# Repeated products at the kernel's begin: 12 of 512 columns in place of 23 of 256

## The chip, the cores and the metric

The kernel runs on one core of a Trainium2 chip. The metric is the device time of one execution in microseconds; the median of three runs stands for the kernel. One further execution was recorded by the hardware profiler, and every line of a profile below comes from such a recorded execution.

## What is computed

The input x is 16 images of 128 channels and 32 x 32 pixels, in float32. Two layers follow each other, and each has a mixing part and a feed-forward part, both added to their input:

```python
# layer 0
x = x + L0_conv(ln_c(x))      # linear attention, 4 heads of 32, over 1024 pixels
t = to_tokens(x)              # (16, 1024, 128)
t = t + L0_ffn(ln_t(t))       # spectral filters: long convolutions with 16 filters, two signs,
                              # each followed by a 128 x 128 matrix, plus 3 taps
# layer 1
x = x + L1_conv(ln_c(x))      # two 3 x 3 convolutions with batch norm and relu
t = t + L1_ffn(ln_t(t))       # routed experts: 64 experts, top 8 tokens each, 128 -> 512 -> 128
```

## The kernel before

The work is one long unrolled program with five stages that follow each other: attention and the forward transforms of layer 0 (to about 381 us), the product stage (to about 652 us), then the inverse transforms with the convolutions and the routing, then the experts, then the output.

The attention stage is a software pipeline over the 16 samples. A tuple `period` (L741) lists the steps of one period with the sample that each works on, written out by hand, and the engines' programs follow it in that order, since the stage is under a manual schedule. Transposes and products write PSUM tiles of the tags "big" (4 KB a partition, three buffers) and "s" (two buffers).

At some points of this order the kernel issues products whose result nobody reads: `keep` (L159) multiplies the identity with itself, repeated along the columns, into a PSUM tile `wm`. The table `idle` (L353) says after which step of which sample, and how many: nine after the `tokens` step of sample 1, eight after the first `filters` step, three after `channels` of sample 0 and three after `k` of sample 1, 23 in all. Two later stages call `keep` with the tag "cv": 26 products ahead of the inverse transforms, some between the routing steps, and four near the end.

The product stage forms, for each of 16 chunks of frequencies, the products of the filters' spectra with the input spectra. Its arrays and steps are:

- `generate(c, q)`: 16 small products (L816) of 32 rows into four PSUM banks `pg`, four times four, each in one of four row groups of PE; this makes a part of the filter matrix g of chunk c.
- `collect`: copies `pg` into `g`, on ACT (L829) and on DVE (L827).
- `multiply(c, m, x, py, fresh)`: 16 products (L840) of 128 rows and 32 columns of weights, g with the input spectra v, into the PSUM tile `py`.
- `turns(c, i)`: POOL prepares v from the loaded spectra xc (L807, L808).
- `combine` and `finish`: DVE and POOL form the result ys, and two transfers store it to yd in DRAM (L861).

In a chunk the loop over m runs four times. Each turn issues two `generate` of the next chunk, then two `multiply` of this one, so that PE alternates between a group of L816 and a group of L840. SP issues the loads of xc (L792, `fetch`) in each chunk: two after `generate` in the turn m = 0, one in m = 2 and one in m = 3. A float32 product is recorded in the trace as two matmul records and two weight-load records of PE, so a group of either line is 64 matmul records and 64 weight loads. The last chunk has no `generate`; then PE runs L840 alone.

The manual schedule of this stage holds for PE, DVE, ACT, POOL and SP: each engine takes its instructions in the order in which the code issues them.

Of the kernel before, what the change touches and what calls it, by code (L numbers as in the profile page):

```python
# [8 lines left out]
F32 = mybir.dt.float32  # L9
# [5 lines left out]
P = 128  # L15
# [54 lines left out]
def metaformer_kernel(ctx: ExitStack, tc: tile.TileContext, io: dict, out: bass.AP):  # L70
# [7 lines left out]
    ident = const.tile([P, P], F32, name="ident")  # L78
# [19 lines left out]
    for n, (g_, b_, m_, v_) in enumerate(((V_G1, V_B1, V_M1, V_V1), (V_G2, V_B2, V_M2, V_V2))):  # L98
# [15 lines left out]
                name=nc.get_next_instruction_name(), ins=[], outs=[], act_func_set_id=EXP_LN  # L114
# [43 lines left out]

    def keep(ps, tag, count):  # L159

        if count:
            wm = ps.tile([P, 2, P], F32, name="wm", tag=tag, bufs={"s": 2, "cv": 3}[tag])
        for _ in range(count):
            nc.tensor.matmul(
                wm, ident, ident.unsqueeze(1).to_broadcast([P, 2, P]), start=True, stop=True
            )

    def transpose_out(pt, src):
# [7 lines left out]
    with ExitStack() as l0:  # L176
# [43 lines left out]
        with ExitStack() as a0:  # L220
# [8 lines left out]
            ps = a0.enter_context(tc.tile_pool(name="aps", bufs=2, space=PSUM))  # L229
# [99 lines left out]
            for h in range(HEADS):  # L329
                s = slice(h * DH, (h + 1) * DH)  # L330
# [19 lines left out]
            def small(shape, name):  # L350
                return work.tile(shape, F32, name=name, tag=name, bufs=5)

            idle = {("tokens", 1): 9, ("filters", 0): 8, ("channels", 0): 3, ("k", 1): 3}  # L353

            class Attention:

# [401 lines left out]
            with tc.manual_schedule(engines=PINNED):  # L758
                for p in range(-reach, B):
                    next(preparing, None)  # L760
                    for name, d in period:
                        b = p + d
                        if name == "filters":
                            next(setting, None)
                            keep(ps, "s", idle.pop((name, 0), 0) if p > -reach else 0)
                        elif 0 <= b < B:
                            if name == "tokens":
                                samples[b] = Attention(b)
                            getattr(samples[b], "q_" if name == "q" else name)()
                            keep(ps, "s", idle.get((name, b), 0))  # L770
                assert next(preparing, None) is None
                for _ in setting:
                    pass
# [160 lines left out]
    with ExitStack() as c1:  # L934
# [6 lines left out]
        ps = cps.enter_context(tc.tile_pool(name="cps", bufs=2, space=PSUM, reuse_waits="tile"))  # L941
# [79 lines left out]
        idle = {(13, "turn"): 4, (13, "pooled"): 8, (15, "logits"): 11, (15, "turn"): 1}  # L1021
# [475 lines left out]
        with tc.manual_schedule(engines=PINNED | {mybir.EngineType.SP}):  # L1497
# [7 lines left out]
            for j in range(2):  # L1505
                nc.sync.dma_start(b2[j * E : (j + 1) * E, :], w2[:, HID, :])
            samples = [None] * B
            keep(ps, "cv", 26)
            for b, name in order:
                if name == "yin":  # L1510
# [128 lines left out]
        ps = c1.enter_context(tc.tile_pool(name="fps", bufs=4, space=PSUM, reuse_waits="tile"))  # L1639
# [175 lines left out]
```

## Time and profile before

| | us |
|---|---|
| median of three runs | 1238.39 |
| lowest and highest | 1237.03, 1242.1 |
| profiled execution, its own time | 1234.8 |
| its span | 1233.0 |
| PE busy, share of the span | 1160.1 (94%) |
| DVE, ACT, POOL busy | 935.7, 724.8, 604.0 |
| L816, PE busy | 142.7 |
| L840, PE busy | 126.7 |
| L164 (`keep`), PE busy, 154 matmul records | 35.1 |
| mean granted clock of PE | 0.991 of full speed |

The page gives the busy time of an engine as the union of its instructions, and for a group of instructions of one line the count, the mean duration of one, and the engine's idle time just ahead of them with what ended it. "issue" stands there when nothing that the profile shows, no semaphore and no transfer, ended it. The chain of waits follows the execution back from its last instruction and names at each step what released it. The timeline shows instructions in order of time, merged where they are alike, with the start, the length and the idle time ahead in square brackets. Of the DMA queues, q1 carries the kernel's own transfers; the queue q8 is called "instruction".

Four runs of L164 lie in the attention stage: they start at 10.50, 19.64, 26.93 and 42.47 us and have 18, 16, 6 and 6 matmul records. The product stage starts on PE at 382.20 us.

### The profile page before, as it was taken

How to read it: one execution, taken by the hardware profiler on the slowest of the kernel's cores; microseconds unless marked ns; L12 is line 12 of the kernel's file. 1: busy time of each engine (PE TensorE's matmuls, PEld its weight loads, DVE VectorE, ACT ScalarE, POOL GpSimd, SP SyncE). 2: the span in 40 equal slices, each digit the busy share in tenths (PEclk: the TensorE clock that was granted, in tenths of full speed). 3: DMA queues.
4: the chain of work that ended last, by engine and by line, in shares of the span. 5: the costliest groups of instructions: out<-in, count | busy, mean ns of one | idle time of the engine just before them, and what ended most of it. 6: DMA issues, size and time to landing. Idle time of an engine off the chain costs nothing.

```text
span 1233.0 us, 34413 instructions
## 1 busy us (share of the span) xinstructions
PE 1160.1 (94%) x14398; PEld 953.7 (77%) x14398; DVE 935.7 (76%) x1944; ACT 724.8 (59%) x1420; POOL 604.0 (49%) x800
## 2 busy tenths in 40 slices
PE   6889999999999999999988999999999999998996
PEld 5677767777777988888887888888888888886453
DVE  5888888888776777777764689898888989885235
ACT  4777787776655777777760445555555555644211
POOL 2436454655568789888882433343343333230003
PEclk9999999999999999999998999999999999999998
DMA  7005335253436243434338511233233321416899
GB/s 282 24 31 168 122 108 162 87 174 108 154 121 181 91 138 134 139 133 139 125 133 283 143 52 53 86 101 121 83 122 106 103 86 69 155 35 234 316 403 380
DMA packets 91243, 175.14 MB, mean 142 GB/s; under 512 B 5968, under 2 KB 42064, under 8 KB 90448
## 3 DMA queue, kind: packets, MB, share of 16 engines
q1 hardware_dynamic: 90448, 170.46, 41.0%
q0 software_dynamic: 640, 2.49, 0.7%
q8 instruction: 113, 1.85, 0.6%
q14 instruction: 42, 0.34, 0.1%
HBM read 110.28 MB, written 62.65 MB: 140 GB/s over the span
## 4 chain that ended last, share of the span: by engine, by line
PE 57%; DVE 22%; issue 11%; ACT 5%; DMA 4%; POOL 1%; SPq 0%; POOLq 0%; ACTq 0%; DVEq 0%
PE pg L816 10%; PE py L840 10%; PE pcv L1012 10%; PE big L638 7%; DVE bst L135 4%; PE big L171 3%; PE big L152 3%; PE big L570 3%; PE big L450 2%; PE big L533 2%; PE big L432 2%; DVE abss L1255 1%; DVE xp L1277 1%; DVE xp L1139 1%; ACT tt L144 1%
## 5 line engine op out<-in xcount | busy, mean ns | idle before, releaser
L1012 PE MATMUL pcv<-v,cw 128*128 128x256 f32 x1152 | 258.2, 380 | 0.8 <-POOL v L1202 0.8
L1012 PEld LDWEIGHTS pcv<-v,cw 128*128 128x128 f32 x1152 | 214.7, 190 | 33.9 <-issue 4.9
L829 ACT COPY g<-pg 128x512 f32<-128x512 f32 x316 | 161.1, 606 | 38.0 <-PE pg L816 37.3
L827 DVE COPY g<-pg 128x512 f32<-128x512 f32 x196 | 127.7, 681 | 68.3 <-PE pg L816 68.3
L816 PE MATMUL pg<-ph,mst 32*128 32x128 f32 x4096 | 142.7, 279 | 5.5 <-issue 4.5
L816 PEld LDWEIGHTS pg<-ph,mst 32*128 32x128 f32 x4096 | 127.9, 186 | 21.4 <-issue 10.7
L840 PE MATMUL py<-g,v 128*32 128x128 f32 x4096 | 126.7, 276 | 3.6 <-issue 2.1
L840 PEld LDWEIGHTS py<-g,v 128*32 128x32 f32 x4096 | 109.8, 111 | 11.7 <-issue 2.4
L144 ACT ACTIVATE tok<-tok,sts 128x128 f32<-128x128 f32 x256 | 101.9, 480 | 16.9 <-DVE sts L1089 13.6
L135 DVE BATCH_NORM_STATS2 bst<-big 128x6 f32<-128x256 f32 x256 | 91.0, 416 | 20.8 <-PE big L152 11.7
L807 POOL TENSOR_TENSOR v<-xc 128x256 f32<-128x256 f32 x128 | 99.9, 803 | 11.5 <-DMA xc<-vd 10.9
L638 PE MATMUL big<-u,mu 128*128 128x128 f32 (+4 forms) x384 | 86.0, 380 | 0.0
L1202 POOL TENSOR_TENSOR v<-abss 128x256 f32<-128x256 f32 x64 | 49.1, 787 | 68.2 <-DVE abss L1198 56.7
L286 POOL TENSOR_TENSOR xf<-ab 128x256 f32<-128x256 f32 x34 | 24.8, 728 | 110.5 <-DVE ab L253 110.5
L1221 POOL TENSOR_TENSOR yo<-abss 128x256 f32<-128x256 f32 x32 | 23.5, 734 | 108.5 <-DVE abss L1217 108.5
L638 PEld LDWEIGHTS big<-u,mu 128*128 128x128 f32 x384 | 56.7, 191 | 18.0 <-issue 15.4
L570 PE MATMUL big<-wf,ub 128*128 128x256 f32 x256 | 62.0, 385 | 0.2
L144 ACT ACTIVATE tt<-tt,sts 128x128 f32<-128x128 f32 x128 | 51.1, 480 | 14.5 <-DVE sts L1089 14.5
L808 POOL TENSOR_SCALAR v<-v 128x256 f32<-128x256 f32 x64 | 55.2, 863 | 5.6
L475 POOL TENSOR_TENSOR ke<-ke,ks 128x1024 f32<-128x1024 f32 x16 | 30.6, 1913 | 55.1 <-DVE qs L483 43.4
L570 PEld LDWEIGHTS big<-wf,ub 128*128 128x128 f32 x256 | 46.2, 190 | 8.8 <-ACT xn L423 3.0
L914 ACT COPY yt<-py 128x512 f32<-128x512 f32 x60 | 35.1, 585 | 27.9 <-ACT g L829 17.2
(256 smaller groups left out, 2488.4 us busy)
## 6 DMA issues: line engine op xcount, KB each, us to landing
we<-in_weight SPq DMA_DIRECT2D x32, 1024.0 KB, 8.9
xc<-vd SPq DMA_DIRECT2D x64, 256.0 KB, 3.2
yd<-ys SPq DMA_DIRECT2D x32, 512.0 KB, 3.5
vd<-xf SPq DMA_DIRECT2D x15, 1024.0 KB, 5.1
y<-yd SPq DMA_DIRECT2D x15, 896.0 KB, 6.2
x<-in_x SPq DMA_DIRECT2D x16, 512.0 KB, 5.2
mi<-in_M_phi SPq DMA_DIRECT2D x16, 512.0 KB, 4.7
xd<-x SPq DMA_DIRECT2D x16, 512.0 KB, 6.3
```

The costliest lines, as they stand in the source:

```text
L135: nc.vector.bn_stats(bst[:, j : j + 2, :].rearrange("p j s -> p (j s)"), src[:, j : j + 2, :].rearrange("p j c -> p c j"),)
L144: nc.scalar.activation(dst[:, j, :], src[:, j, :], AF.Identity, bias=nm[:, j : j + 1], scale=r[:, j : j + 1],)
L570: nc.tensor.matmul(dst, self.ub[:, q, :], wf[:, q, :], start=True, stop=True)
L638: nc.tensor.matmul(self.pa[:, a:hi], mu[:, NF - 1 - si, tap, :], self.u[:, a - tap : hi - tap], start=(tap == 0), stop=(tap == KU - 1),)
L807: nc.gpsimd.tensor_tensor(vv[:, x, 1:, bs], e, o, op)
L808: nc.gpsimd.tensor_scalar(v[:, :, 0, bs], v[:, :, 2, bs], -1.0, None, ALU.mult)
L816: nc.tensor.matmul(pg[r][:, i], mst[rs, 4 * q + i, :], ph[rs, c, :], start=True, stop=True,)
L827: nc.vector.tensor_copy(dst, src)
L829: nc.scalar.copy(dst, src)
L840: nc.tensor.matmul(py[rows, x, kl, :], v[:, (x * NM + m) * JL + jl, 1 - ri : 3 - ri, :] .rearrange("p k b -> p (k b)"), g[:, ((x * 2 + ri) ...
L1012: nc.tensor.matmul(pc[:, i], wt[:, dy, k, :], v[:, k, dy * WT : dy * WT + HT], start=(dy == 0), stop=(dy == 2),)
L1202: nc.gpsimd.tensor_tensor(v[:, k, WT : WT + HT], self.ab[:, 0], self.ab[:, 1], op)
```

## The change

The PSUM tile of `keep` and the columns of one product depend on the tag now: four times 128 columns with the tag "s", which the attention stage uses, and two times 128 with "cv", as it was. The table `idle` of the attention stage has 5, 4, 1 and 2 products in place of 9, 8, 3 and 3: 12 of 512 columns (6144 in all) in place of 23 of 256 (5888). The number of buffers of each tag is as before. In the program this takes away 11 products, 44 instructions of PE, ahead of the product stage; the other engines' instructions and their order are unchanged.

```diff
     def keep(ps, tag, count):
 
+        n, bufs = {"s": (4, 2), "cv": (2, 3)}[tag]
         if count:
-            wm = ps.tile([P, 2, P], F32, name="wm", tag=tag, bufs={"s": 2, "cv": 3}[tag])
+            wm = ps.tile([P, n, P], F32, name="wm", tag=tag, bufs=bufs)
         for _ in range(count):
             nc.tensor.matmul(
-                wm, ident, ident.unsqueeze(1).to_broadcast([P, 2, P]), start=True, stop=True
+                wm, ident, ident.unsqueeze(1).to_broadcast([P, n, P]), start=True, stop=True
             )
...
-            idle = {("tokens", 1): 9, ("filters", 0): 8, ("channels", 0): 3, ("k", 1): 3}
+            idle = {("tokens", 1): 5, ("filters", 0): 4, ("channels", 0): 1, ("k", 1): 2}
```

## The prediction

> **What bounds the kernel now.** I read the page's shares first, then its groups, then the chain of waits, then the timeline of the stage that the chain names. PE is busy 94% of the span and the chain is 57% PE, led by two lines of the product stage:
>
> ```profile
> PE 57%; DVE 22%; issue 11%; ACT 5%; DMA 4%; POOL 1%; SPq 0%; POOLq 0%; ACTq 0%; DVEq 0%
> ...
> L816 PE MATMUL pg<-ph,mst 32*128 32x128 f32 x4096 | 142.7, 279 | 5.5 <-issue 4.5
> ...
> L840 PE MATMUL py<-g,v 128*32 128x128 f32 x4096 | 126.7, 276 | 3.6 <-issue 2.1
> ```
>
> Their idle time is put down to "issue": PE had operands and buffers, and still did not go. The PE timeline shows where:
>
> ```profile
> 427.50 2.07 PE L816 MATMUL pg<-ph,mst 32*128 32x128 f32 x64
> 429.50 1.95 PE L840 MATMUL py<-g,v 128*32 128x128 f32 x64
> 431.38 2.07 PE L816 MATMUL pg<-ph,mst 32*128 32x128 f32 x64
> 433.38 1.96 PE L840 MATMUL py<-g,v 128*32 128x128 f32 x64
> 435.26 2.18 PE L816 MATMUL pg<-ph,mst 32*128 32x128 f32 x64
> 437.37 1.95 PE L840 MATMUL py<-g,v 128*32 128x128 f32 x64
> 439.25 0.94 PE L816 MATMUL pg<-ph,mst 32*128 32x128 f32 x20
> 440.38 0.84 PE L816 MATMUL pg<-ph,mst 32*128 32x128 f32 x20 [0.19 <-issue]
> ```
>
> One L816 group and one L840 group take 2.00 + 1.88 = 3.88 us undisturbed (427.50 to 431.38). The 439.25 group is broken after 20 products and reaches L840 at 441.92: 2.67 us instead of 2.00. The 435.26 group took 2.11. This repeats every chunk (four pairs): breaks at 424.08, 440.38, 456.69, 473.00, 489.31. From the L816 start at 399.68 to the one at 636.55 there are 58 pairs; 58 x 3.88 = 225.0 us, the trace shows 236.9, so **11.8 us are lost**, 0.81 a chunk.
>
> The broken places are periodic in the count of instructions. Numbering all PE records (products, weight loads, semaphore records) in order, every "issue" wait of the stage lies at number 193 or 194 modulo 256, while the start of the group drifts. The page has a queue that moves blocks of that size:
>
> ```profile
> q8 instruction: 113, 1.85, 0.6%
> ```
>
> 1.85 MB / 113 = 16 KB, and 28,981 PE records / 113 = 256. So PE's own instructions arrive in blocks of 256, and the stage eats a block in 3.88 us. The packet records give the delivery: a packet starts at least 1.05 us after PE has crossed into the block before, takes 0.97, and a stalled PE goes on 1.31 to 1.45 after it landed (landed 439.01, on at 440.38). But often it starts later, and then its start follows the kernel's transfers:
>
> ```profile
> 430.15 0.80 SPq L792 DMA_DIRECT2D xc<-vd  x2
> 434.29 0.80 SPq L861 DMA_DIRECT2D yd<-ys  x2
> 438.69 4.57 SPq L792 DMA_DIRECT2D xc<-vd  x2
> ```
>
> After a yd pair the block's packet starts 3.70 to 3.82 us behind the first issue (434.29 to 438.06) in nearly all chunks, although the crossing lay anywhere from 1.4 to 1.9 us behind it; after an xc pair 3.3 to 3.5; after a single xc about 2.2, mostly within the 1.05. Four packets, a chunk's worth, take 16.3 us, against 15.5 of PE work.
>
> [...] The windows view shows a mean of 0.91 over 60 to 70 us, behind the 2.72 us wait for wy at 67.33.
>
> **The change part by part.** (1) Products at the begin, L164 (46 of its 154 records). A 256-column product is two records 0.216 us apart; a 512-column one two at 0.45 (L432: four from 31.28 to 33.08). PE pays 46 x 0.216 = 9.9 us before and 24 x 0.45 = 10.8 after. None lies on the path: run 1 goes from 10.50 to about 15.0, phi lands at 15.98 (idle then 1.56); run 2 from 19.64 to 23.3, then gt until 24.25; run 3 shrinks 1.3 to 0.9 ahead of xn at 29.25; run 4 grows 1.3 to 1.8, from 42.47 to 44.3, ahead of gt at 44.74. 0 us. If that cover were gone, run 4 would cost 0.5. [...]
> (2) The wm tile grows to 2 KB a partition with the same two buffers. The instruction order of the two kernels is equal on DVE, ACT, POOL and SP, and on PE but for these rows, with the same waits: 0 us.
> (3) 11 products fewer are 22 matmul and 22 weight-load records: **every block boundary falls 44 records later in the work.** In the L816 group it moves from record 41 to 85 (early chunks) and from 27 to 71 (late ones; a few semaphore records shift it). Inside the group a record is 13.1 ns, so PE reaches the boundary 0.57 us later, while the yd and xc issues hang on the work and stay.
> Walk one undisturbed chunk, G = start of an L816 group. yd pair at G - 0.97, packet at G + 2.80, usable at G + 2.80 + 0.95 + 1.35 = 5.10, which is 1.22 into the next group. Before, PE is at the boundary 0.67 in: it waits. After, 1.24 in: the wait vanishes early; late (1.06 in) 0.16 is left. xc pair: issued G - 1.23, packet G + 2.2, usable 0.6 to 0.7 into the next group: even before, free after. The other two: crossing at 1.22 at the latest + 1.05 + 0.97 + 1.35 = 0.71 into the next group, free.
> A wait costs its length plus a restart of 0.2 to 0.3 (440.38: 0.37 longer than usual, 0.67 lost), a block just in time about 0.1 (435.26). So a chunk loses 0.1 early and about 0.4 late, mean 0.23, against 0.81. The same rule carried through the 58 pairs with their own packet times gives 11.7 before (trace 11.8) and 3.3 after. **Gain 8.4 us.**
> (4) Last chunk: the wait "issue" of 2.10 us before 647.30 ends with a packet that starts at 645.02 behind the loads of 639 to 641 (wi, 1024 KB, at 641.01). PE gets there 44 x 14.7 ns = 0.65 later: gain 0.65. It may also spare the half clock that follows it (0.89 over 636.6 to 652.4), at most 1.7; not counted.
> (5) Elsewhere: in the attention, convolution and expert stages a block lands 3.5 to 29 us before PE needs it. 0. The wait at 395.25 is followed by one for v (POOL, behind the xc loads) until 398.02, so shortening it gains 0.
> Sum 9.1 us. The profiled execution took 1234.8 us (span 1233.0 and 1.8 around it): 1225.7. It lies 3.6 under the median of the runs, 1238.4; that median becomes 1229.3.
>
> What is late next is POOL:
>
> ```profile
> core 0: us, PE busy (x) PEld busy (x) DVE busy (x) ACT busy (x) POOL busy (x), PEclk, DMA share, GB/s
> ...
> 457.00:473.30 16.30, 16.10 (x519) 14.64 (x516) 12.12 (x20) 12.52 (x24) 14.05 (x17) 1.00 0.40 133
> ```
>
> 14.05 of 16.30 us; a chunk of 15.6 still holds it, and the first pairs ran four times at 3.88 without a break.
>
> **Rivals.** *The fetch keeps a rhythm of its own* (four blocks in 16.3 us wherever the boundary lies): gain 0, 1238.4. For it: chunk and four blocks have the same period, so most chunks can't tell. Against: the constant distance to yd. *Gain taken up elsewhere*: if POOL's turns or the xc loads allow no chunk below 15.9, 0.4 x 14.5 = 6 is gained, 1232. Against: POOL waits 1.5 us a chunk for DVE's ys. *Not the count that decides*, or not 44: also 1238.4; the order listing speaks against it. *Slower*: a fetch asked for later runs into the next single xc (issued G + 3.0, just ahead of the next group) and waits for it: packet G + 5.2, usable 3.6 into the next group, a wait of 2.4, against 0.81 now; in all 14.5 chunks +23 us, 1261. It decides from about 5 chunks on. Against: that packet starts near G + 2.3, 0.7 us ahead.
>
> **How the numbers follow.** Forecast, or more: 0.68 (a gain over 6.2 us, which is 0.5%, about what a measurement of this kernel can tell from no change). Gain taken up: 0.12, own rhythm or wrong count 0.15, both within 0.5%; slower 0.05. Low end: all 11.8 and most of the last wait and its clock, 14.4, gives 1224; high end: no change and 1 us of spread, 1239.5.
>
> **What would show it.** Right: "issue" waits stay at the same number modulo 256 but lie some 40 products into L816; pairs mostly 3.88 us apart; the 58 pairs take about 228 us; L816's idle for issue falls. Wrong: breaks every 16.3 us as now; packets no longer tied to yd; PE idle in the stage for DVE, ACT or POOL; or a new idle in the first 60 us.

## The result, and the profile after

The median is 1232.87 us (20 runs, 1226.33 to 1240.06) against 1236.96 for the kernel before in the same comparison. The ratio is **0.9959, with an interval of 0.9943 to 0.9976**: 5.1 us gained, between 3.0 and 7.0. The forecast was 9.1 us. The profiled execution took 1229.23 us (span 1227.4) against 1234.8 (span 1233.0), 5.6 less. Line numbers below `keep`'s new line are one higher than before: L816 is L817, L840 is L841.

From the page of the kernel after, the shares of its chain of waits and the two groups of the product stage:

```profile
PE 54%; DVE 21%; issue 10%; ACT 6%; DMA 5%; POOL 2%; SPq 0%; POOLq 0%; ACTq 0%; DVEq 0%
...
L817 PE MATMUL pg<-ph,mst 32*128 32x128 f32 x4096 | 138.6, 278 | 1.1 <-DVE x L646 0.9
L841 PE MATMUL py<-g,v 128*32 128x128 f32 x4096 | 125.1, 274 | 2.4 <-POOL v L809 1.8
```

Before, 4.5 of the 5.5 us of idle time ahead of the first group and 2.1 of the 3.6 ahead of the second were put down to "issue"; now 1.1 and 2.4 us are left, most of it put down to DVE and POOL. PE's timeline at the place where the kernel before broke at 440.38, again start, length and idle time in brackets:

```profile
430.13 2.07 PE L817 MATMUL pg<-ph,mst 32*128 32x128 f32 x64
432.12 1.96 PE L841 MATMUL py<-g,v 128*32 128x128 f32 x64
434.01 2.17 PE L817 MATMUL pg<-ph,mst 32*128 32x128 f32 x64
436.11 1.95 PE L841 MATMUL py<-g,v 128*32 128x128 f32 x64
438.00 2.07 PE L817 MATMUL pg<-ph,mst 32*128 32x128 f32 x64
439.99 1.95 PE L841 MATMUL py<-g,v 128*32 128x128 f32 x64
```

No group is broken. One takes 2.17 in place of 2.07: its block of instructions had landed 1.46 us before PE went on in it, within the 1.24 to 1.48 us after which PE went on at the 18 gaps over 0.15 us that the kernel before has at block boundaries, so it came just in time. Later in the stage such groups stand close together:

```profile
568.10 2.22 PE L817 MATMUL pg<-ph,mst 32*128 32x128 f32 x64
...
572.14 2.38 PE L817 MATMUL pg<-ph,mst 32*128 32x128 f32 x64
...
576.34 2.33 PE L817 MATMUL pg<-ph,mst 32*128 32x128 f32 x64
```

From the L817 group at 399.08 to the last one at 628.29, 58 pairs, the stage takes 229.21 us in place of 236.87. At 3.8815 us for an undisturbed pair (3.88 in the prediction) the loss fell from 11.75 to 4.08.

**The last chunk** gained as well. Before:

```profile
641.05 4.15 PE L840 MATMUL py<-g,v 128*32 128x128 f32 x141 [0.54 <-DVE pooled L927]
647.30 5.13 PE L840 MATMUL py<-g,v 128*32 128x128 f32 x115 [2.10 <-issue]
```

After:

```profile
633.21 4.55 PE L841 MATMUL py<-g,v 128*32 128x128 f32 x155 [0.56 <-POOL v L809]
638.20 2.82 PE L841 MATMUL py<-g,v 128*32 128x128 f32 x93 [0.43 <-issue]
640.94 11.49 PE L165 MATMUL wm<-ident 128*128 128x256 f32 x52
```

The wait for instructions fell from 2.10 to 0.43, and the half clock behind it (granted clock 0.50 from 648.4 to 651.8 before) is not there (1.00 from 633.0 to 656.0). From the last L817 group to the L165 run (`keep` with "cv", behind the stage) it is 12.65 us in place of 15.81. With 0.6 gained ahead of the first pair, the stage ends 11.43 us earlier (640.94 against 652.37). Neither the 0.6 nor the 3.2 is firm: five more executions with the same count of PE records (experiments 2, 5, 6, 7 and 9) start the first pair 0.4 to 1.5 us later than the kernel before, and in experiment 2 the wait in the last chunk is back.

**The transition** to the convolutions then takes back 4.6 of these 11.4 us. The chain of waits before:

```profile
656.18 4.33 DMA yd<-ys
...
663.56 9.91 DMA cw<-cwd
673.48 9.95 DMA y<-yd
...
688.01 5.45 PE pcv L1012 x24
```

After:

```profile
644.77 7.31 DMA yd<-ys
...
655.11 10.50 DMA cw<-cwd
665.63 11.01 DMA y<-yd
...
681.20 5.45 PE pcv L1013 x24
```

The stage's last yd pair is issued 11.4 us earlier but takes 7.31 us to land instead of 4.33; SP issues nothing of what follows until then (its next transfer is at 652.53, before at 660.98). Then the loads of cw and y take 0.6 and 1.1 longer. The last line of each fence begins with the 13th matmul record of the convolutions, called the 13th record below; it starts only 6.8 us earlier. The windows view, from the begin of the L164 or L165 run to that record, before and then after (time, then busy time and count of PE, PEld, DVE, ACT and POOL, the granted clock, the share of the DMA engines, GB/s):

```profile
652.37:688.01 35.64, 29.82 (x169) 25.59 (x168) 19.55 (x40) 7.92 (x15) 11.29 (x15) 0.95 0.89 269
```

```profile
640.94:681.20 40.26, 29.87 (x171) 25.89 (x169) 19.98 (x40) 7.92 (x15) 11.30 (x15) 0.96 0.92 267
```

PE's work is the same, the rate is the same, each has one stretch of 3.4 us at half clock (granted clock 0.50 from 668.9 before, from 656.0 after), and there is more to move: 35.64 us at 269 GB/s is 9.59 MB, 40.26 at 267 is 10.75. The 1.16 MB more take 4.3 us at this rate, and the stretch is 4.6 longer. They are probably for the most part the loads of xp and y (1.4 MB) that POOL issues during the last chunk. POOL's timeline before and after:

```profile
646.51 0.62 POOL L1032 DMA_DIRECT2D xp<-xd  x1
647.13 0.69 POOL L1035 DMA_DIRECT2D y<-yd  x1
```

```profile
638.44 0.62 POOL L1033 DMA_DIRECT2D xp<-xd  x1
639.05 0.69 POOL L1036 DMA_DIRECT2D y<-yd  x1
```

Before, they are issued 5.9 us ahead of the stage's end and 9 ahead of the last yd pair (655.82); after, 2.5 and 6 us ahead (644.41). From the issue of the pair to its landing the DMA engines moved 1.1 MB before (233 GB/s from 655.8 to 660.5) and 2.05 after (270 from 644.4 to 652.0), and the pair itself is 1.05, so that it seems to share them with these loads for longer; experiment 9 tests that. From the 13th record on, the convolutions and the routing run alike (425.7 and 425.8 us to the last record of a convolution). Behind POOL's last step in the chain, which ends 6.85 us earlier (1217.39 against 1224.24), the program still runs 10.0 us instead of 8.8, and 5.6 us reach the end.

### The profile page after: what moved, and what is told of

Its sections match the earlier page's. It is cut to its first block, busy times and chain, and to the rows that moved or that the text cites. A ratio compares the mean times of both kernels' runs of the same rounds, so it can differ in the third digit from the quotient of the medians.

```text
span 1227.4 us, 34369 instructions
## 1 busy us (share of the span) xinstructions
PE 1154.2 (94%) x14376; PEld 945.1 (77%) x14376; DVE 930.1 (76%) x1944; ACT 725.1 (59%) x1420; POOL 601.0 (49%) x800
## 4 chain that ended last, share of the span: by engine, by line
PE 54%; DVE 21%; issue 10%; ACT 6%; DMA 5%; POOL 2%; SPq 0%; POOLq 0%; ACTq 0%; DVEq 0%
PE pg L817 10%; PE pcv L1013 10%; PE py L841 10%; PE big L639 6%; DVE bst L135 4%; PE big L172 3%; PE big L152 3%; PE big L571 3%; PE big L451 2%; PE big L534 2%; PE big L433 2%; DVE abss L1256 1%; DVE xp L1278 1%; DVE xp L1140 1%; ACT ub L550 1%
## 5 line engine op out<-in xcount | busy, mean ns | idle before, releaser
L817 PE MATMUL pg<-ph,mst 32*128 32x128 f32 x4096 | 138.6, 278 | 1.1 <-DVE x L646 0.9
L817 PEld LDWEIGHTS pg<-ph,mst 32*128 32x128 f32 x4096 | 125.9, 186 | 14.8 <-DVE g L828 8.3
L841 PE MATMUL py<-g,v 128*32 128x128 f32 x4096 | 125.1, 274 | 2.4 <-POOL v L809 1.8
L841 PEld LDWEIGHTS py<-g,v 128*32 128x32 f32 x4096 | 108.1, 110 | 10.6 <-POOL v L809 2.3
L808 POOL TENSOR_TENSOR v<-xc 128x256 f32<-128x256 f32 x128 | 97.0, 781 | 11.2 <-DMA xc<-vd 10.6
L1203 POOL TENSOR_TENSOR v<-abss 128x256 f32<-128x256 f32 x64 | 49.0, 786 | 68.2 <-DVE abss L1199 56.7
```

Source lines behind the costliest of these rows:

```text
L808: nc.gpsimd.tensor_tensor(vv[:, x, 1:, bs], e, o, op)
L817: nc.tensor.matmul(pg[r][:, i], mst[rs, 4 * q + i, :], ph[rs, c, :], start=True, stop=True,)
L841: nc.tensor.matmul(py[rows, x, kl, :], v[:, (x * NM + m) * JL + jl, 1 - ri : 3 - ri, :] .rearrange("p k b -> p (k b)"), g[:, ((x * 2 + ri) ...
L1203: nc.gpsimd.tensor_tensor(v[:, k, WT : WT + HT], self.ab[:, 0], self.ab[:, 1], op)
```

## The experiments

My theory was that the place of the 256-record boundaries in the work, and so the count of PE records ahead of the stage, decides the pairs, and that the transition is bound by bytes. The rivals: the size of the products or of the tile, a rhythm of the fetch's own, and PE's time in the last chunk. "Pairs" below is the time of the 58 pairs, and "entry" the time from the start of the last L817 group to the 13th record (51.46 before, 52.91 after). All ratios are to the kernel before. The diffs show the lines that matter; where a loop over `ticks` is added, a table gives its count behind each step. Times inside a kernel come from one execution of each.

**1. The count put back** in the kernel after, with products of one column: four behind `tokens`, three behind `filters`, four behind `channels`, so that the 11 products are there again and the columns hardly change.

```diff
+        for _ in range(ticks):
+            nc.tensor.matmul(wm[:, 0, 0:1], ident, ident[:, 0:1], start=True, stop=True)
```

> The changed kernel with 11 one-column products more at its begin: PE's columns and PSUM tile as after the change, the count of PE records ahead of the product stage as before it (boundary again at record 41 to 27 of the L816 group). If the count decides, the 58 pairs of the product stage take 236 to 238 us again and the time is that of the kernel before, ratio 0.998 to 1.002. If the wider products or the clock at the begin decide, the pairs take about 229 us and the ratio stays near 0.996. If the four blocks had a rhythm of their own, the pairs would show 16.3 us in four wherever the boundary lies.

Ratio 1.0005 (0.9989 to 1.0020); pairs 236.28. The breaks are back, at the same kind of place as in the kernel before; the page of this kernel:

```profile
L823 PE MATMUL pg<-ph,mst 32*128 32x128 f32 x4096 | 142.9, 279 | 4.4 <-issue 3.4
```

With the 44 records back the pairs take what they took before, so the gain hangs on the count, and neither the 512 columns nor the larger tile brings one. This kernel enters the stage 1.7 us later than the kernel before (383.91), which is in its ratio.

**2. Twelve products of 256 columns**, the other half of that test: the count of after, half the columns and the old tile.

```diff
-        n, bufs = {"s": (4, 2), "cv": (2, 3)}[tag]
+        n, bufs = {"s": (2, 2), "cv": (2, 3)}[tag]
```

> 12 products of 256 columns: the count of the changed kernel, half its columns. If the count decides: pairs near 229 us, product stage ended some 10 us earlier than in the kernel before, ratio 0.994 to 0.998 as after the change. If PE's work at the begin decides: another time[...].

Ratio 0.9958 (0.9942 to 0.9973), pairs 229.91: as the kernel after, although PE has 10.8 / 2 = 5.4 us less to do at the begin. This run tells something of the transition as well. In its last chunk the wait for instructions is back:

```profile
641.41 2.82 PE L841 MATMUL py<-g,v 128*32 128x128 f32 x93 [1.80 <-issue]
644.16 6.09 PE L165 MATMUL wm<-ident 128*128 128x256 f32 x27
```

So its stage ends 3.2 us later than that of the kernel after, 14.12 us behind the last L817 group in place of 12.65, and yet its 13th record starts at 681.20, the same as there.

**3. and 4. More records in the kernel before**, 28 and 13 products of one column (10, 8, 7, 3 and 5, 4, 4, 0 behind the four steps), the `ticks` loop as in 1. The boundary comes to lie in the L840 group, at record 57 to 43 with 28 and at 117 to 103 with 13.

> The kernel before with 28 one-column products more at its begin, 112 records: the boundary falls at record 57 to 43 of the L840 group (185 to 171 of the pair). The rule of the prediction gives no wait at all in the 58 pairs: 225 to 226 us, against 236.9 before and 229.2 after; ratio 0.990 to 0.995 if the gain is kept behind the stage. Added products cost nothing if the waits at the begin cover them, up to 3 us if not. If a boundary in the L840 group costs more than in L816, the pairs take longer than 229.

> The kernel before with 13 one-column products more, 52 records: the boundary falls at record 117 to 103 of the L840 group, just ahead of the single xc issue. The rule says that the request then runs into that transfer and the next block comes late: waits of over 1 us in every chunk, 58 pairs in 245 to 260 us, ratio 1.005 to 1.02, with 15 products less than the run beside it. If only the direction of the shift counted, or if the rule of the request and the transfers is wrong, the time lies between that of the kernel before and 0.4% below.

With 28: ratio 0.9944 (0.9925 to 0.9964), pairs 225.44, nothing but 0.3 us lost. It begins the stage 3.7 us late (385.87), since the added products take longer at the begin (2.29, 1.84, 1.62 and 0.72 us in their four runs) than the waits there cover and PE is at half clock for 3.4 us from 18.9 (the 16 records with phi take 5.39 us there, 3.69 before), and is still faster than the kernel before. With 13: **1.0107 (1.0083 to 1.0131), slower**, pairs 251.06. Its timeline:

```profile
442.95 1.93 PE L846 MATMUL py<-g,v 128*32 128x128 f32 x58
445.70 0.42 PE L846 MATMUL py<-g,v 128*32 128x128 f32 x6 [0.82 <-issue]
```

L846 is this kernel's L840. PE stops after 58 of the 64 records. With fifteen products of one column fewer than in 3 it is 20 us slower: a size of work can't do that, nor can a rhythm of the fetch's own, which would give all kernels the same pairs. The table that follows has this kernel's break at 445.70, behind a yd pair, but not all are of that kind: of the 32 gaps over 0.15 us between the two PE records at a block boundary in the 58 pairs (18 in the kernel before, 6 after), 14 have a single xc load as the transfer issued last ahead of the packet, 10 a yd pair and 8 an xc pair.

**The same block in six kernels.** From the packet records of q8 and the SP and PE timelines, for PE's record 8129, which is where the kernel before breaks at 440.38. "Into the block before" is when PE crossed the boundary before this one. Times but the last column count from the issue of the yd pair ahead of it:

| kernel | into the block before | packet starts | landed | PE reaches the boundary | PE's gap there, us |
|---|---|---|---|---|---|
| before | 1.63 | 3.77 | 4.72 | 5.63 | 0.46 |
| count back (1) | 1.63 | 3.79 | 4.72 | 5.51 | 0.67 |
| 13 added (4) | 1.14 | 4.06 | 5.00 | 5.15 | 1.09 |
| after | 2.19 | 3.65 | 4.61 | 6.08 | 0.09 |
| 24 added (8) | 0.09 | 1.38 | 2.31 | 3.88 | 0.09 |
| 28 added (3) | -0.14 | 0.07 | 1.30 | 3.65 | 0.09 |

0.09 is the usual distance of two groups of records. In this block the packet comes within 1.4 us of the yd issue when PE crosses up to 0.09 us behind that issue; where PE crosses 1.14 or more behind it, the packet starts 3.7 to 4.1 behind the issue, whether the crossing was 1.1 or 2.2 us behind it. Then it matters when PE wants the block: at 5.2 to 5.6 it waits, at 6.1 it doesn't. By the place of the boundary, from early chunks to late ones, the 58 pairs lose 11.8 us at L816 record 41 to 27, 4.1 at 85 to 71, 0.3 at L840 record 57 to 43, 0.2 at 73 to 59, and 25.9 at 117 to 103. So the change went most of the way down; the lowest losses measured lie 100 to 116 records further on (a pair has 256), and another 44 records on is the highest. No run kept the count and moved these transfers: that the packet follows them is read from these distances.

**5. PE slowed in the last chunk** of the kernel after by 16 products of 128 columns.

```diff
+                        for _ in range(4 if c + 1 == NCH else 0):
+                            nc.tensor.matmul(py[:, 0, 0, :], ident, ident, start=True, stop=True)
                         for x in range(2):
```

> The changed kernel with 16 products of the identity more in the last chunk, which nobody reads: some 3.5 us of PE time ahead of the last multiplies, about what the change gained in this chunk (12.65 us from the last pair to the end of the stage, against 15.81 before). If transfers bind from there on (the last yd pair lands behind the loads of xp and y that were issued 6 us ahead of it), the end of the stage moves 2.5 to 3.5 us later, the last yd pair lands in less than 7.3 us, the convolution starts (13th product of pcv, at 681.20 after the change) within 1.5 us of before this edit, and the ratio stays at 0.995 to 0.997. If the end of the stage decides, the convolution starts 3 us later and the ratio is near 0.999.

From the last L817 group to the L165 run it is 15.98 us, 3.3 more. The ratio is 0.9946 (0.9926 to 0.9966), not shown to differ from the kernel after, and entry is 52.32 in place of 52.91. The chain:

```profile
649.63 4.74 DMA yd<-ys
...
657.40 9.77 DMA cw<-cwd
667.18 10.37 DMA y<-yd
```

The yd pair lands in 4.74 again. The 3.2 us that the change gained in the last chunk bring nothing as far as the 13th record, as experiment 2 shows too: a stage that ends earlier only meets more of the loads.

**6. and 7. The loads of cw ahead of the others** on SP, in the kernel after, both of them in 6 and only the first in 7. The diff is that of 6:

```diff
+            for n in range(2):
+                nc.sync.dma_start(cw[n], cwd[n])
             for b in range(2):
                 load(b)
-            for n in range(2):
-                nc.sync.dma_start(cw[n], cwd[n])
```

> The changed kernel with both loads of cw (1152 KB each) issued by SP ahead of the loads of the first two samples, so that they no longer queue behind the wait for the last yd pair. If idle DMA time between yd and y costs the transition (57 and 95 GB/s in the two 2.5 us slices from 650 to 655), the convolution starts 1 to 4 us sooner and the ratio falls to 0.992 to 0.995. If sample 0's y, which then waits behind 2.3 MB, decides, the first product with wi comes 2 to 4 us later than 655.9 and the convolution starts 0 to 3 us later: 0.996 to 0.999. It can also be neither, when SBUF of cw comes free only at the stage's end.

> As the run with both cw loads first, but only cw0 is moved, cw1 stays behind the samples. If the idle DMA time is the cost, the 1152 KB fit into it and sample 0's y is hardly later: convolution 1 to 3 us sooner, ratio 0.993 to 0.995. If y of sample 0 or the transfers' own rate decides, no change: 0.995 to 0.997.

Ratios 0.9997 (0.9984 to 1.0009) and 0.9960 (0.9942 to 0.9979): the first loses the gain and lies above both ranges expected, the second shows no change. The chain of 6:

```profile
646.99 13.41 DMA yd<-ys
660.45 3.15 DMA y<-yd
```

cw is issued before the last yd pair now and goes through at its cost: the pair takes 13.41 us (10.79 in 7), and entry is 55.06 (51.56 in 7). The transfer that was moved ahead took its time from the next one.

**8. The kernel before with 24 cheap products**: as in 3, but with 32 columns of weights, and 8, 6, 7 and 3 of them: the eight behind `filters` took 1.84 us in 3, the eight behind `tokens` take 0.67 here.

```diff
+        for _ in range(ticks):
+            nc.tensor.matmul(wm[:32, 0, 0:1], ident[:, :32], ident[:, 0:1], start=True, stop=True)
```

> The kernel before with 24 products of 32 columns of weights and one column more at its begin, 96 records, shorter than those of the run with 28: the boundary falls at record 73 to 59 of the L840 group. By the rule no wait in the 58 pairs, 225 to 226 us as with 28, and the stage begins sooner than with 28 (385.87 there, 382.2 before). If the 58 pairs decide what the change is worth: ratio 0.990 to 0.994, below both the changed kernel and the run with 28. If the transition takes the rest back, 0.994 to 0.996.

Pairs 225.35; the stage begins at 382.22, as in the kernel before. Ratio **0.9919 (0.9887 to 0.9950)**, median 1226.96 (7 runs) against 1235.94: the lowest ratio of these kernels, 10 us below the kernel before (6 to 14), though its interval overlaps those of the others that gain. On its page neither group has issue as its main wait:

```profile
L846 PE MATMUL py<-g,v 128*32 128x128 f32 x4096 | 125.3, 274 | 3.1 <-POOL v L814 1.8
L822 PE MATMUL pg<-ph,mst 32*128 32x128 f32 x4096 | 135.1, 277 | 0.9 <-DVE x L649 0.9
```

Its last pair starts 11.65 us earlier than before (624.90), and the 13th record 8.8 (679.20): it pays at the transition as well (entry 54.30). It pays once more right behind that:

```profile
679.20 7.64 PE L1018 MATMUL pcv<-v,cw 128*128 128x256 f32 x24 [4.92 <-POOL v L1208]
```

The 24 records that took 5.45 us in the kernels before and after take 7.64, with PE at half clock for 6.8 us from 676.9 on, within the wait (the mean granted clock from 638.32 to the 13th record is 0.93, before 0.95). The last record of a convolution is then only 6.5 us earlier than before. So this execution, which ends 6.5 us before that of the kernel before and 0.9 before that of the kernel after, does not show the 10 us of the ratio.

**9. POOL's two loads moved to SP**, in the kernel after, so that they stand behind the last yd pair.

```diff
-            (nc.sync if b else nc.gpsimd).dma_start(xt[b], xd[b])
+            nc.sync.dma_start(xt[b], xd[b])
...
-                (nc.gpsimd if b + i == 0 else nc.sync).dma_start(
+                nc.sync.dma_start(
```

> The kernel after, with the loads of sample 0 that POOL issues (xp, and the first part of y) issued by SP instead, so that they stand behind the last yd pair and not ahead of it. PE's instructions and the product stage are unchanged: pairs about 229 to 231 us. Theory A (the last yd pair takes 7.3 us in the kernel after because these loads, issued 6 us ahead of it, share its transfer time): the pair lands in 4.3 to 4.8 us, SP goes on about 3 us earlier; but the bytes taken from ahead of it now follow it, so the 13th pcv product lies 51 to 55 us behind the last pair (52.9 in the kernel after), ratio 0.993 to 1.000. Rival B (the pair is long for another reason, such as its own size or the stage's other stores): it still takes about 7 us, SP's later loads start no earlier, and the 13th pcv product lies 3 us or more later, since xp and y now start 14 us later; ratio 0.998 to 1.003.

The chain:

```profile
645.81 3.94 DMA yd<-ys
649.81 6.77 DMA y<-yd
```

The pair takes 3.94 in place of 7.31, so these loads were what it shared with. Entry is 49.87, 3.0 better than after and a little better than either theory had it; the 10.85 MB from the L165 run to the 13th record go at 286 GB/s, where the kernel after moved 10.75 MB at 267. So the bytes alone do not set the length of this stretch: their order counts too. But the ratio is 0.9955 (0.9934 to 0.9976), as the kernel after. The table follows four kernels to the end, in us from the span's start:

| | last pair | 13th record | last record of a convolution | end of the span |
|---|---|---|---|---|
| before | 636.55 | 688.01 | 1113.74 | 1232.99 |
| after | 628.29 | 681.20 | 1106.97 | 1227.41 |
| POOL's loads on SP (9) | 630.06 | 679.93 | 1104.96 | 1229.81 |
| 24 added (8) | 624.90 | 679.20 | 1107.25 | 1226.47 |

In 9, the part behind the last convolution (experts and output) took 124.9 us, against 119.2 to 120.4 in the other three, with PE at half clock for 6.8 us from 1194.1 (mean granted clock 0.85 from 1180 to 1200; the other three are at 1.00 there and at 0.91 from 1120 to 1140, where 9 is at 1.00). Whether that follows from the order of the loads, or is the spread of single executions, stays open; so does what the 3.0 us are worth at the end.

## Why the prediction was right in kind and too large

**The mechanism held.** Experiments 1, 3 and 4 change the count of PE records by tiny products, and the pairs follow it from 225.4 to 251.1 us, in both directions; in experiment 2 the count stays, and so do the pairs. In the kernels that wait, the waits lie at the same record number modulo 256: 193 or 194 in the prediction, and the six gaps over 0.15 us that the kernel after has at block boundaries lie there too.

**Step 1 and step 2, nothing at the begin: right.** The product stage starts at 382.06 us, before at 382.20, and in experiment 2, with half the columns and the old tile, at 382.14. No half clock is added ahead of the stage, one is gone: the 0.91 of the prediction comes from a granted clock of 0.50 from 68.2 to 71.5, and after it is 1.00 from 60 to 70, although the wait for wy at 67.31 is 2.71 us long there too.

**Step 3, the pairs: 7.7 us measured, 8.4 predicted.** The walk through the packet times left a loss of 3.3, the trace shows 4.08. The first 28 pairs lose 0.66, the other 30 lose 3.42: late in the stage up to three blocks in a row come just in time (568 to 578 above). The walk also called the packets behind a single xc load free, and of the six gaps over 0.15 us that are left at block boundaries, four have one issued 0.2 to 0.3 us ahead of the packet. Its figures for the fetch were off there: the last part of this document has the floor of 1.05 us, and behind a single xc load the packets of the kernel before start 2.0 to 3.2 us later, 2.6 in the middle, where the prediction says about 2.2. The five other executions with this count have pairs of 228.9 to 231.3, so that the agreement to 0.7 us is no closer than their spread.

**Step 4, the last chunk: 0.65 predicted, 3.2 measured,** since the wait fell to 0.43 and the half clock of 3.4 us, which the text put at 1.7 and did not count, is not there. The prediction let the packet stand where it was and PE come later; in fact the packet starts 1.4 us behind the issue of the load of wi in place of 4.0. That is in part luck, for in experiment 2, with the same count, it starts 4.3 behind it, and this stretch is 14.12 long. Experiments 2 and 5 show that the size does not matter for the 13th record.

**The step that failed is the sum.** It carried the 9.1 us of the product stage to the end of the program as if the next stage started as soon as this one is done, and asked only of POOL what would be late next. POOL was not: it is busy 13.4 to 13.7 us of a chunk of 15.52. Late next were the transfers between the stages. The profile before had it in view: its chain showed yd, cw and y in a row from 656.18 on. Along the profiled executions, the last pair starts 8.3 us earlier, close to the 8.4 predicted, though by luck: the 0.6 ahead of the first pair, which the prediction put at nothing, makes up for what the pairs lack. The 13th record starts 6.8 earlier, since the 3.2 of the last chunk are lost and 1.45 more; and 5.6 reach the end. That the last chunk does not count is shown by experiments 2 and 5. That the rest of the 4.6 us is lost to transfers is what the bytes of the two windows account for, and experiment 9, which wins 3.0 of it back by their order, supports it; in experiment 2 entry is 51.17, no worse than before, so the 1.45 are not a firm size. The last 1.2 us lie at the program's end, where no run took them apart.

**The rivals.** The fetch's own rhythm falls with experiment 4, a wrong count with experiment 1. "Gain taken up elsewhere" is what happened, but at the transition and not by POOL or the xc loads inside a chunk. The slower rival, a request that runs into the next single xc load, did not decide this change; experiment 4 shows an alignment where it is at work and the kernel is 13 us slower. There 14 of the 32 gaps lie behind a single xc load, all but one with packets 2.1 to 3.3 us behind its issue; 18 lie behind the pairs of yd and xc, which the rival did not name.

## What to carry to other kernels

When PE idles for "issue" at a fixed distance in records, count the records to the next block boundary (256 records a block here) and compare it with the transfers issued just before. Ahead of this loop 13 tiny products cost 13 us and 24 gained some 10 by the ratio, so try several counts. A gain in one stage need not reach the end, since the next stage's first transfers can be the bound: here 11.4 us at the stage's end were 6.8 at the 13th record. Multiply the rate by the length of that stretch, before and after, see whether the bytes explain it, and then whether another order of the transfers changes the rate.

## What the runs showed of the hardware

The prediction took 1.05 us from PE's crossing to the start of the next block's packet as a floor. It is none. In the kernel before itself, 9 of the 58 packets start 0.22 to 0.91 us behind the crossing; where PE crossed at 400.25 and 404.13, 8.4 and 12.3 us after the last transfer was issued, it was 0.41 and 0.22, and in the other seven a single xc load was the last transfer. In experiments 3 and 8, with the boundary in the L840 group, most packets start 0.1 to 0.7 us behind the crossing. The crossings of these two also lie elsewhere among the transfers: in the kernels before and after, 53 and 54 of the 58 crossings lie 0.9 to 2.5 us behind the last issue of a transfer, and in experiments 3 and 8 none does; there PE crosses as the transfers are issued or over 2.5 us behind them. A transfer of xc takes 3.2 us and one of yd 3.5 from issue to landing on the page of the kernel before. So the distance seems to follow the transfers under way rather than the place in the group; no run tried that by itself.

The waits for blocks cost these 58 pairs, each a block of 3.88 us of work, 0.2 us in experiment 8, 4.1 in the kernel after, 11.8 before and 25.9 in experiment 4: how much of them shows is a matter of alignment here.
